# Handing layer 1's expert results to layer 2's attention batch by batch, and agreeing the maxima of a quantized attention through TensorE

## The chip, the cores and the metric

The kernel runs on one core of a Trainium2 chip. The metric is the device time of one execution in microseconds (us). A core has five engines that matter here: PE (TensorE, matrix products and transposes), DVE (VectorE), ACT (ScalarE), POOL (GpSimd) and SP (SyncE, which only issues transfers). Each works through its own list of instructions in order; an instruction waits until what it reads is there and what it overwrites is free, and everything behind it on the same engine waits with it. PEld is the loading of weights into PE, which overlaps its matmuls.

## The reference, cut to what matters

The whole is a decoder of four layers with three sublayers each, on X of 8 batches, 256 tokens and 256 features, always x = layernorm(x + sublayer(x)). The change touches the hand-over from the third sublayer of layer 1 (routed experts) to layer 2, the attention of layer 2, and its second sublayer, which is quantized.

```python
# layer 1, experts: each token takes the rows of its 4 experts, weighted
routed = zeros_like(x).at[t_s].add(expert_out[e_s, slot] * gate)
x = layernorm(x + routed + shared)
# layer 2, attention: 16 heads, causal; then the quantized sublayer
def bitnet_linear(x, W, b):
    w_scale = maximum(mean(abs(W)), 1e-05)
    qW = sign(W) * (abs(W) > 0.5 * w_scale)
    i_scale = maximum(max(abs(x)), 1e-08) / 127.0      # one maximum over ALL of x
    qx = clip(round(x / i_scale), -128.0, 127.0)
    return einsum('...i,oi->...o', qx, qW) * (w_scale * i_scale) + b
vis = bitnet_linear(dinov2_features, W_d2v, b_d2v)
image_embeds = bitnet_linear(vis, W_img, b_img)
fused = bitnet_linear(text_embeddings, W_txt, b_txt)   # text_embeddings is x
for Wa, ba in ((W_att0, b_att0), (W_att1, b_att1)):
    kv = bitnet_linear(image_embeds, Wa, ba)
    k = concatenate([kv, kv], axis=-1)
    attn = softmax(einsum('bse,bpe->bsp', fused, k) * inv_sqrt_e, axis=-1)
    fused = fused + 0.1 * einsum('bsp,bpe->bse', attn, k)
concatenated = concatenate([fused, broadcast(mean(image_embeds))], axis=-1)
h = relu(bitnet_linear(concatenated, W_f1, b_f1))
x = layernorm(x + bitnet_linear(h, W_f2, b_f2))
```

Six inputs of `bitnet_linear` need a maximum over everything: the context (called ctx in the code), vis, the image embeddings (img), x, the concatenation (cat) and the hidden layer (hid).

## The kernel before, in words

X stays in SBUF as 128 partitions by 16 tiles by 256 features (tile t holds tokens 128t to 128t+127; a batch is two tiles). `xT` is its transposed copy: four PE transposes (L175) and one ACT copy (L176) for two tiles. The sublayers run one after the other, but a planner orders the instructions on each engine by estimated costs and due times, so work of the next sublayer stands where an engine has room. Matrix products go through the helper `mm` (L134), and so many groups of the profile carry that line.

*Norms.* `finish_x` takes statistics with DVE (L165, L166), then 1/sqrt(variance) for two tiles by `rsqrt`, then writes X (L189). `rsqrt` has two forms: where `self.power` is set, two POOL instructions, an addition (L143) and a power (L145); otherwise eleven small DVE instructions (L148, L150, and three times L153, L154, L156). `POWER` lists the sublayers with the POOL form; the quantized sublayer is not among them.

*Experts of layer 1 to layer 2.* The 32 experts write their rows to DRAM (`yd1`). Inside the expert loop, `prepare_l2_xattn` also runs: it turns the weights of the quantized sublayer into -1, 0, 1 and computes vis, img and the transposed keys `l2x_kvT`. Afterwards `routed_batches` returns two functions to the attention: `gather(b)` fetches a batch's expert rows with eight indirect DMAs issued by POOL (helper at L953), `take(b)` multiplies the selection matrix with the gates (L1282, DVE), sums the rows by PE (L1291), adds to X (L1296) and norms. The buffer `ys` holds the rows of four tiles, that is two batches, by tile number modulo 4.

*Attention.* `attention16` projects a pair of batches (`pair`), then per batch: the largest score of each row (`largest16`, DVE reduces L499 and L515, lowered into q by L534 and L536), exponentials (`exps16`, ACT, L554), weighted sums (`sums16`, PE L603, then divisions on POOL L590, the addition with bias on POOL L612, and the norm). Scores of b+1 go between the exponentials of b. Before the first projection it gathers batches 0 and 1, takes both, and issues the gathers of 2 and 3 behind each take; later `gather(b + 4)` stands at the head of iteration b and `take(b + 3)` behind the second exponential step.

*Maxima.* `all_max` reduces along the free dimension with DVE (L1766) and over the 128 partitions with POOL's all-reduce (L1768). `step_of` makes the step, its inverse and the scales (L1776 to L1782), `quantize` rounds 512 columns with two DVE instructions (L1790, L1791), `bit_linear_T` multiplies and adds scale and bias (L1867).

*Quantized sublayer* (`l2_xattn`). x's maximum is taken of all of `xT` in one reduce over 128x4096. Then 16 calls of `bit_attend` (two rounds of eight batches): the keys' transpose (L1963, PE) and its copy (L1965, ACT), scores of two tiles (PE), the row maximum (L1971), subtraction (L1973), exponential (ACT), sum (L1976), reciprocal (L1977), multiplication (L1978), two transposes (L1981), copy (L1983), product (PE), and the addition to `fused` (L1987). Then the maximum of `fused` in one reduce (L1889), the maximum of the 8x256 averages (L1890), cat's all-reduce, 16 quantizations, a first pass over the hidden layer that keeps only maxima (`top`, L1921), hid's all-reduce, and four chunks of 512 tokens: hidden layer again, Relu on ACT (L1939), quantization, second product, addition to z (z = X + b2 on POOL, L1949; L1956 on DVE), norm.

## Time and profile before

| | |
|---|---|
| median of 3 runs | 2708.56 us (2705.01 to 2714.05) |
| profiled execution | 2698.26 us, its span 2696.5 us |
| mean granted TensorE clock | 0.886 of full speed |
| experts of layer 1 end, first gathers begin | 1108 to 1111 us |
| first projection of layer 2's attention | 1154.55 us |
| last write of X in that attention | 1408.12 us, 0.73 us long for both tiles |
| first multiplications with x's step | 1419.52 us |
| 16 calls of `bit_attend` | 1431.5 to 1473.6 us |
| maximum of fused | 1473.62 us, 4.42 us long |
| hid's all-reduce | 1516.78 us |
| last X of the quantized sublayer | about 1576 us |

Times of instructions count from the start of the span. A row of the timeline gives start, duration, engine, line, operation, output<-input with the names of the program, shapes, and in brackets the engine's idle time before it with what released it; "issue" is idle time for which the profile shows no cause. A group sums all instructions of one line and form: busy us, mean ns of one, and idle time ahead of them. The chain of waits is followed back from the last instruction of the span.

### The profile page before, as it was taken

What the parts mean: (1) busy time and instruction counts of PE and PEld (TensorE: products, weight loads), DVE (VectorE), ACT (ScalarE), POOL (GpSimd) and SP (SyncE); (2) the same over time, 40 slices, a digit from 0 to 9 for tenths busy, and PEclk for the clock granted to TensorE, in tenths of its full rate; (3) what the DMA queues carried; (4) which work ended last, traced back from release to release, by engine and by line L of the source; (5) the groups of instructions that cost most, each with busy time, mean ns of one, the idle gap of its engine ahead of it and who ended that gap; (6) DMA issues with size and microseconds to landing.
All of it is one profiled execution on the core that took longest, in us unless ns stands there. A gap on an engine that the chain in (4) does not pass through costs nothing.

```text
span 2696.5 us, 41126 instructions
## 1 busy us (share of the span) xinstructions
PE 2157.2 (80%) x14463; PEld 1564.6 (58%) x14463; DVE 1624.2 (60%) x5567; ACT 987.7 (37%) x2234; POOL 935.2 (35%) x980
## 2 busy tenths in 40 slices
PE   8988789699988688667976777778788778777796
PEld 5656678455565477334544355556667656565575
DVE  4764200566667575246667886758667676654675
ACT  2322233233433332123432343344435434343563
POOL 1021221311111134443110145665566555662122
PEclk9998799799988689778997888889889989887899
DMA  2002431200010137411010021111111111120000
GB/s 83 2 1 65 174 128 56 71 1 1 1 67 17 49 111 228 121 56 32 1 50 10 1 66 44 42 49 44 41 43 42 47 43 41 51 72 16 0 13 20
DMA packets 84173, 135.05 MB, mean 50 GB/s; under 512 B 33445, under 2 KB 53045, under 8 KB 82048
## 3 DMA queue, kind: packets, MB, share of 16 engines
q0 software_dynamic: 52288, 79.27, 10.0%
q1 hardware_dynamic: 28924, 49.45, 5.5%
q10 hardware_dynamic: 2756, 3.72, 0.4%
q8 instruction: 115, 1.88, 0.3%
q14 instruction: 90, 0.74, 0.1%
HBM read 242.90 MB, written 17.70 MB: 97 GB/s over the span
## 4 chain that ended last, share of the span: by engine, by line
PE 36%; DVE 22%; issue 10%; POOL 5%; ACT 4%; DMA 3%; another core or an unknown queue 3%; POOLq 0%; ACTq 0%; DVEq 0%
PE po L1498 5%; PE pp L134 4%; PE sc L134 4%; PE s L134 4%; DVE low L515 2%; DMA xe<-xd,take 2%; PE ph L134 2%; PE sc L482 2%; PE pt L134 2%; DVE low L499 2%; PE sc L603 2%; DVE junk L1446 1%; POOL rows L953 1%; DVE X L189 1%
## 5 line engine op out<-in xcount | busy, mean ns | idle before, releaser
L953 POOL DMA_INDIRECT rows<-in_l2f_table_dram,index x512 | 532.3, 1040 | 337.7 <-issue 121.5
L1498 PE MATMUL po<-rows,diag 128*128 128x256 f32 x768 | 231.8, 440 | 105.1 <-ACT diag L1497 68.1
L1446 DVE SCALAR_TENSOR_TENSOR junk<-rows,X 128x256 f32<-128x256 f32 x512 | 214.8, 420 | 53.4 <-DMA rows<-in_l2f_table_dram,index 32.4
L1498 PEld LDWEIGHTS po<-rows,diag 128*128 128x128 f32 x768 | 155.5, 216 | 156.4 <-ACT diag L1497 82.4
L134 PE MATMUL pp<-xT,w 128*128 128x256 f32 (+1 forms) x672 | 199.5, 436 | 30.6 <-issue 20.4
L134 PE MATMUL ph<-xeT,we 128*128 128x128 f32 x1248 | 182.1, 289 | 19.4 <-DMA we<-in_l0f_experts_dram,wrow 15.0
L590 POOL TENSOR_TENSOR aT<-sides,inv 128x256 f32<-128x256 f32 x64 | 46.7, 730 | 425.8 <-DVE sides L588 310.8
L134 PEld LDWEIGHTS ph<-xeT,we 128*128 128x128 f32 x1248 | 168.5, 199 | 39.3 <-DMA we<-in_l0f_experts_dram,wrow 16.3
L1497 ACT ACTIVATE diag<-ident,dots 128x128 f32<-128x128 f32 x384 | 134.3, 395 | 117.8 <-PE po L1498 48.1
L134 PEld LDWEIGHTS pp<-xT,w 128*128 128x128 f32 x672 | 139.5, 216 | 61.9 <-issue 25.8
L175 PE MATMUL pt<-ident,X 128*128 128x128 f32 x352 | 75.9, 330 | 107.0 <-DVE X L189 89.1
L953 POOL DMA_INDIRECT xe<-xd,take x87 | 85.0, 977 | 204.1 <-DVE y L1074 77.6
L176 ACT COPY xT<-pt 128x512 f32<-128x512 f32 x88 | 51.6, 586 | 271.6 <-PE pt L175 232.4
L175 PEld LDWEIGHTS pt<-ident,X 128*128 128x128 f32 x352 | 49.9, 164 | 140.3 <-DVE X L189 51.6
L134 PE MATMUL py<-we,hT 128*128 128x256 f32 x496 | 129.0, 384 | 0.9 <-DVE hT L1097 0.9
L1074 DVE TENSOR_TENSOR y<-py,we 128x256 f32<-128x256 f32 x23 | 9.8, 425 | 197.5 <-PE py L134 197.5
L554 ACT ACTIVATE e<-sc 128x512 f32<-128x512 f32 (+1 forms) x154 | 81.4, 602 | 103.0 <-PE sc L482 74.2
L1068 ACT ACTIVATE hT<-ph,we 128x128 f32<-128x128 f32 x184 | 65.7, 367 | 119.5 <-PE ph L134 87.9
L482 PE MATMUL sc<-kv,qv 32*128 32x128 f32 (+2 forms) x1448 | 103.9, 320 | 1.8 <-DVE qv L700 0.6
L189 DVE TENSOR_SCALAR X<-z,ln_mv,rs_y 128x256 f32<-128x256 f32 x176 | 68.3, 431 | 51.5 <-POOL rs_y L145 51.3
L482 PEld LDWEIGHTS sc<-kv,qv 32*128 32x128 f32 x1448 | 80.4, 190 | 31.4 <-issue 26.0
L482 PE MATMUL sc<-qv,kv 32*128 32x128 f32 (+2 forms) x1384 | 97.0, 343 | 0.1
(510 smaller groups left out, 5150.3 us busy)
## 6 DMA issues: line engine op xcount, KB each, us to landing
we<-in_l1f_experts_dram SPq DMA_DIRECT2D x32, 384.0 KB
yd<-y SPq DMA_DIRECT2D x32, 256.0 KB
rows<-in_l2f_table_dram,index POOLq DMA_INDIRECT x512
w<-in_l2x_w_dram SPq DMA_DIRECT2D x1, 4096.0 KB
yd<-y SPq DMA_DIRECT2D x23, 128.0 KB
X<-in_x_dram SPq DMA_DIRECT2D x8, 256.0 KB
xd<-X ACTq DMA_DIRECT2D x8, 256.0 KB
xd<-X SPq DMA_DIRECT2D x8, 256.0 KB
```

Of the source, the lines that this page charges most:

```text
L134: self.nc.tensor.matmul(out, lhsT=lhsT, rhs=rhs, start=n == 0, stop=n == last and bias is None)
L175: nc.tensor.transpose(pt[:, c, j, :], self.X[:, i0 + j * step, c * P : (c + 1) * P], self.ident)
L189: nc.vector.tensor_scalar(self.X[:, i, :], z[:, j, :], mv[:, j, 0:1], r[:, j : j + 1], ALU.subtract, ALU.mult)
L482: nc.tensor.matmul(sc[: shape[0], part], lhsT=lhsT, rhs=rhs, start=mask is None, stop=True, skip_group_check=True)
L499: nc.vector.tensor_reduce(low5[:, r, :, :, 0], sc, AX.X, ALU.max, negate=True)
L515: nc.vector.tensor_reduce(low4[:, r, :, 0], sc, AX.X, ALU.max, negate=True)
L554: lambda r, sc: nc.scalar.activation(e0[m][:n0, r], sc, AF.Exp),
L953: self.nc.gpsimd.indirect_dma_start(out=out, out_offset=None, in_=table, in_offset=bass.IndirectOffsetOnAxis(ap=index, axis=0), **({} if r ...
L1068: nc.scalar.activation(hT[:, g + f, :], ph[:, f, :], AF.Gelu, bias=b1[:, g + f : g + f + 1])
L1446: nc.vector.scalar_tensor_tensor(junk, row, 1.0, self.X[:, i, :], ALU.mult, ALU.mult, accum_out=out)
L1497: nc.scalar.activation(diag, self.ident, AF.Copy, scale=dots[:, k : k + 1])
L1498: nc.tensor.matmul(po, lhsT=diag, rhs=rows[:, k, D:], start=False, stop=g + k == H * K - 2)
```

## The change

1. `routed_batches` returns three functions instead of two. `first` gathers batches 0 and 1, takes both, and issues the gathers of batch 2 behind the take of batch 0; `second`, after the first projection, takes batch 2 and issues the gathers of batch 3; `inside(b)` takes b+3 and only then gathers b+4. Batch 1's rows lie in the second half of `ys`, those of all other batches in the first half, so that a batch's gathers follow its predecessor's sum. Norms of batches 0 and 1 take the DVE form of `rsqrt`.
2. `all_max` transposes the column of 128 maxima with PE, reduces the row with DVE, and spreads the one value over the partitions by a matmul with a row of ones. All six maxima use it.
3. x's maximum is collected by batches during layer 2's attention (`measure`, a reduce over 128x512 of X behind each norm), fused's during the second round of `bit_attend`.
4. The 16 transposes of the keys and their copies (now four of 128 columns by four) move from `bit_attend` to `prepare_l2_xattn`, into layer 1's expert loop; `l2x_kv` keeps them.
5. `bit_attend`: the negative scaled maximum becomes the bias of the exponential, which ACT takes from PSUM in two instructions that also give the sums; subtraction and sum on DVE go.
6. Loops over 512 columns become the outer ones in `quantized`, `bit_linear_T` and for the input of f1.
7. The quantized sublayer joins `POWER`.

```diff
@@ -84,6 +84,8 @@
         self.avg = self.const.tile([P, 2, B], F32, name="avg")
+        self.x_max = self.const.tile([P, B], F32, name="x_max")
         self.w_scale = self.const.tile([P, len(L2X)], F32, name="w_scale")
@@ -640,18 +643,10 @@
-        if ready:
-            gather, take = ready
-            for b in range(2):
-                gather(b)
-            for b in range(2):
-                take(b)
-                self.transpose_into_xT(2 * b, 1)
-                gather(b + 2)
+        first, second, inside = ready or (lambda: None, lambda: None, lambda b: (lambda: None,) * 3)
+        first()
         pair(0)
-        if ready:
-            take(2)
-            self.transpose_into_xT(4, 1)
+        second()
         for step in self.largest16(q[0], k[0], low[0], sizes, causal):
@@ -661,22 +656,21 @@
             here, e = self.exps16(q[b], k[b], sizes, causal, work)
-            if ready and b + 4 < B:
-                gather(b + 4)
+            early, late, last = inside(b)
+            early()
             for n, step in enumerate(here):
...
                     ahead[n]()
-                if n == 1 and ready and b + 3 < B:
-                    take(b + 3)
+                if n == 1:
+                    late()
                 if n == 0 and before:
...
                 before[1]()
-            if ready and b + 3 < B:
-                self.transpose_into_xT(2 * b + 6, 1)
+            last()
             values = vps[b // 2 % 2]
@@ -789,6 +783,12 @@
         nc = self.nc
+        def measure(b):
+            nc.vector.tensor_reduce(
+                self.x_max[:, b : b + 1], self.X[:, 2 * b : 2 * b + 2, :], AX.XY, ALU.max, apply_absolute_value=True
+            )
         wq, wkd, wku, wo, bku, bo, spare = w
@@ -810,7 +810,7 @@
-            self.attention16(project, low, vps, [P, P], True, wo, bo, work, ready=self.routed_batches(spare))
+            self.attention16(project, low, vps, [P, P], True, wo, bo, work, then=measure, ready=self.routed_batches(spare))
@@ -1273,9 +1273,13 @@
         def gather(b):
-            for t in (2 * b, 2 * b + 1):
+            for j in range(2):
+                t = 2 * b + j
                 for g in range(4):
-                    self.gather_rows(ys[:, t % 4, g, :], self.yd1, self.slot1[:, t, g : g + 1])
+                    self.gather_rows(ys[:, rows_at(b) + j, g, :], self.yd1, self.slot1[:, t, g : g + 1])
+        def rows_at(b):
+            return 2 if b == 1 else 0
@@ -1289,14 +1293,44 @@
                     nc.tensor.matmul(
-                        po[bands[g], j, :], lhsT=sel[:, j, g, :], rhs=ys[:, (2 * b + j) % 4, g, :],
+                        po[bands[g], j, :], lhsT=sel[:, j, g, :], rhs=ys[:, rows_at(b) + j, g, :],
                         start=True, stop=True, skip_group_check=True,
...
             nc.vector.tensor_tensor(x, po, x, ALU.add)
+            self.power = b > 1
             self.finish_x(2 * b, 1, x)
-        return gather, take
+            self.power = True
+        def first():
+            for b in range(2):
+                gather(b)
+            for b in range(2):
+                take(b)
+                self.transpose_into_xT(2 * b, 1)
+                if not b:
+                    gather(2)
+        def second():
+            take(2)
+            gather(3)
+            self.transpose_into_xT(4, 1)
+        def inside(b):
+            def late():
+                if b + 3 < B:
+                    take(b + 3)
+                if b + 4 < B:
+                    gather(b + 4)
+            def last():
+                if b + 3 < B:
+                    self.transpose_into_xT(2 * b + 6, 1)
+            return lambda: None, late, last
+        return first, second, inside
@@ -1759,14 +1793,19 @@
-    def all_max(self, parts, pool, name):
+    def all_max(self, parts, pool, name, bank=None):
...
         nc.vector.tensor_reduce(m, parts, AX.X, ALU.max, apply_absolute_value=True)
-        out = pool.tile([P, 1], F32, name=f"{name}_all")
-        nc.gpsimd.partition_all_reduce(out, m, P, bass_isa.ReduceOp.max)
-        return out
+        bank = bank or (lambda: self.ps_t.tile([P, 512], F32, name="pt"))
+        pt = bank()[:1, :P]
+        nc.tensor.transpose(pt, m, self.ident)
+        out = pool.tile([1, 1], F32, name=f"{name}_all")
+        nc.vector.tensor_reduce(out, pt, AX.X, ALU.max)
+        pt = bank()[:, :1]
+        nc.tensor.matmul(pt, lhsT=self.ones, rhs=out, start=True, stop=True)
+        return pt
@@ -1821,13 +1860,13 @@
-    def quantized(self, q, src, name, into, work, *weights):
+    def quantized(self, q, src, name, into, work, *weights, largest=None, bank=None):
         n = src.shape[2]
-        m = self.all_max(src.rearrange("p c n -> p (c n)"), into, name)
+        m = self.all_max(src.rearrange("p c n -> p (c n)") if largest is None else largest, into, name, bank)
         inv, scales = self.step_of(m, [q[x][1] for x in weights], into, name)
         dst = into.tile([P, 2, n], BF16, name="q_act")
-        for c in range(2):
-            for o in range(0, n, 512):
+        for o in range(0, n, 512):
+            for c in range(2):
                 e = min(o + 512, n)
@@ -1836,20 +1875,29 @@
         q = self.l2x_q = self.ternary(pool)
+        bank = lambda: ps.tile([P, 512], F32, name="pp")
         half = self.l2x_flat[:, 4096 : 4096 + 2 * NCTX]
         self.l2x_kvT = half.rearrange("p (c n) -> p c n", c=2)
         vis = pool.tile([P, 2, NCTX], F32, name="vis")
-        qc, (s,) = self.quantized(q, self.ctxT, "ctx", pool, pool, "d2v")
+        qc, (s,) = self.quantized(q, self.ctxT, "ctx", pool, pool, "d2v", bank=bank)
         self.bit_linear_T(vis, q["d2v"][0], qc, s, self.col("l2x_b_d2v"), ps)
         img = pool.tile([P, 2, NCTX], F32, name="img")
-        qv, (s,) = self.quantized(q, vis, "vis", pool, pool, "img")
+        qv, (s,) = self.quantized(q, vis, "vis", pool, pool, "img", bank=bank)
         self.bit_linear_T(img, q["img"][0], qv, s, self.col("l2x_b_img"), ps)
-        qi, scales = self.quantized(q, img, "img", pool, pool, "att0", "att1")
+        qi, scales = self.quantized(q, img, "img", pool, pool, "att0", "att1", bank=bank)
         for n in range(2):
...
             )
+        self.l2x_kv = self.l2x_flat[:SC, 6144:8192].rearrange("p (a n) -> p a n", n=P)
+        for n in range(2):
+            for b in range(0, B, 4):
+                pt = bank()[:SC].rearrange("p (a n) -> p a n", n=P)
+                for a in range(4):
+                    nc.tensor.transpose(pt[:, a, :], self.l2x_kvT[:, n, (b + a) * SC : (b + a + 1) * SC], self.ident)
+                nc.scalar.copy(self.l2x_kv[:, n * B + b : n * B + b + 4, :], pt)
         nc.vector.tensor_reduce(self.avg, img.rearrange("p c (b s) -> p c b s", s=SC), AX.X, ALU.add)
@@ -1857,8 +1905,8 @@
         n = src.shape[2]
-        for m in range(dst.shape[1]):
-            for o in range(0, n, 512):
+        for o in range(0, n, 512):
+            for m in range(dst.shape[1]):
                 e = min(o + 512, n)
@@ -1877,22 +1925,28 @@
             fused = pool.tile([P, 2, NTOK], F32, name="fused")
+            largest = pool.tile([P, B + 1], F32, name="largest")
+            nc.vector.tensor_reduce(largest[:, B:], avg, AX.XY, ALU.max, apply_absolute_value=True)
             if True:
                 with tc.tile_pool(name="x2a", bufs=3, space=PSUM) as ps:
-                    qx, (s,) = self.quantized(q, self.xT, "x", pool, work, "txt")
+                    qx, (s,) = self.quantized(q, self.xT, "x", pool, work, "txt", largest=self.x_max)
                     self.bit_linear_T(fused, q["txt"][0], qx, s, self.col("l2x_b_txt"), ps)
...
                         for b in range(B):
-                            self.bit_attend(fused, kvT[:, n, b * SC : (b + 1) * SC], b, work, ps)
-            largest = pool.tile([P, 2], F32, name="largest")
-            nc.vector.tensor_reduce(largest[:, 0:1], fused, AX.XY, ALU.max, apply_absolute_value=True)
-            nc.vector.tensor_reduce(largest[:, 1:2], avg, AX.XY, ALU.max, apply_absolute_value=True)
+                            self.bit_attend(
+                                fused, kvT[:, n, b * SC : (b + 1) * SC], self.l2x_kv[:, n * B + b, :], b, work, ps
+                            )
+                            if n:
+                                nc.vector.tensor_reduce(
+                                    largest[:, b : b + 1], fused[:, :, b * S : (b + 1) * S], AX.XY, ALU.max,
+                                    apply_absolute_value=True,
+                                )
             m = self.all_max(largest, pool, "cat")
             inv, (s1,) = self.step_of(m, [q["f1"][1]], pool, "cat")
             qf = pool.tile([P, 2, NTOK], BF16, name="q_act")
-            for c in range(2):
-                for o in range(0, NTOK, 512):
+            for o in range(0, NTOK, 512):
+                for c in range(2):
                     self.quantize(qf[:, c, o : o + 512], fused[:, c, o : o + 512], inv, work)
@@ -1956,24 +2010,22 @@
-    def bit_attend(self, fused, kvb, b, work, ps):
-        nc = self.nc
-        pt = self.ps_t.tile([SC, P], F32, name="pt")
-        nc.tensor.transpose(pt, kvb, self.ident)
-        kv = work.tile([SC, P], F32, name="kv")
-        nc.scalar.copy(kv, pt)
+    def bit_attend(self, fused, kvb, kv, b, work, ps):
+        nc = self.nc
         sc = ps.tile([P, 2, SC], F32, name="sc")
...
         nc.vector.tensor_reduce(mx, sc, AX.X, ALU.max)
+        nc.vector.tensor_scalar(mx, mx, -(D**-0.5), None, ALU.mult)
         e = work.tile([P, 2, SC], F32, name="e")
-        nc.vector.tensor_tensor(e, sc, mx.unsqueeze(2).to_broadcast([P, 2, SC]), ALU.subtract)
-        nc.scalar.activation(e, e, AF.Exp, scale=D**-0.5)
         total = work.tile([P, 2], F32, name="total")
-        nc.vector.tensor_reduce(total, e, AX.X, ALU.add)
+        for j in range(2):
+            nc.scalar.activation(
+                e[:, j, :], sc[:, j, :], AF.Exp, scale=D**-0.5, bias=mx[:, j : j + 1], accum_out=total[:, j : j + 1]
+            )
         nc.vector.reciprocal(total, total)
@@ -2140,7 +2192,7 @@
-POWER = ("l0_attn", "l0_xattn", "l1_attn", "l1_xattn", "l2_attn")
+POWER = ("l0_attn", "l0_xattn", "l1_attn", "l1_xattn", "l2_attn", "l2_xattn")
```

## The prediction

> **What bounds the kernel now.** I read the page's first part, then the chain that ended last (it names the work that sets the end, stage by stage), then busy time by stretches, groups and single instructions in the stages that the diff touches.
>
> ```profile
> PE 2157.2 (80%) x14463; PEld 1564.6 (58%) x14463; DVE 1624.2 (60%) x5567; ACT 987.7 (37%) x2234; POOL 935.2 (35%) x980
> ```
>
> TensorE (PE) leads with 80% of the span, but no step of the change lightens it by more than a few us. What the change can win are serial stretches, where the chain hops between engines. The first is the hand-over from layer 1's experts to layer 2's attention (columns: start, us, what):
>
> ```profile
> 1108.38 2.12 DMA yd<-y
> 1111.36 0.94 POOL w L953
> ...
> 1130.11 2.58 DMA w<-yd,w
> 1132.89 1.07 PE sc L1291 x2
> 1135.90 2.68 issue
> 1142.62 0.96 POOL w L953
> ...
> 1148.91 0.95 POOL w L953
> 1151.35 0.75 POOL rs_y L145
> 1152.65 1.24 PE pt L175 x4
> 1154.55 3.80 PE sc L134 x4
> ```
>
> The reader is to see POOL (GpSimd) in the middle of it: sixteen gathers of 0.95 us, a start every 1.25 us, before batch 0 and 1 are summed; eight more (batch 2's and half of batch 3's follow on the same queue) before POOL gives the second norm's root at 1151.35 and the first projection starts at 1154.55. The second kind of serial stretch is the agreement of a maximum over partitions (timeline; in brackets the idle time before and its releaser), together with two rows on a shared port, used under part 7:
>
> ```profile
> 1410.64 4.42 DVE L1766 TENSOR_REDUCE x_m<-xT 128x1 f32<-128x4096 f32 x1 [1.57 <-ACT xT L176]
> 1418.73 0.38 POOL L1768 PARTITION_ALL_REDUCE x_all<-x_m  x1 [10.64 <-issue]
> 1419.14 0.15 DVE L1776 TENSOR_SCALAR x_step<-x_all 128x1 f32<-128x1 f32 x1 [4.08 <-POOL x_all L1768]
> ...
> 1516.78 0.38 POOL L1768 PARTITION_ALL_REDUCE hid_all<-hid_m  x1 [5.83 <-issue]
> 1538.81 1.33 POOL L1949 TENSOR_TENSOR z<-X,b 128x512 f32<-128x512 f32 x1 [3.81 <-DVE X L189]
> 1538.92 1.50 DVE L1790 TENSOR_SCALAR quant<-h,hid_inv 128x512 f32<-128x512 f32 x1
> ```
>
> POOL's own work is 0.38 us; ahead of it lie 3.67 us (1415.06 to 1418.73) and 5.5 us (hid_m ends 1511.26) with nothing recorded. The third is the quantized attention of layer 2 and the chunks behind it (stretch, its us, then PE, PEld, DVE, ACT, POOL busy, clock granted to TensorE, DMA share, GB/s), with two groups of VectorE (DVE) and one of TensorE from there:
>
> ```profile
> 1431.50:1452.00 20.50, 17.72 (x122) 15.00 (x122) 16.63 (x50) 7.29 (x24) 0.00 (x0) 1.00 0.01 2
> 1518.00:1550.00 32.00, 23.81 (x128) 12.90 (x129) 31.19 (x111) 21.16 (x44) 4.19 (x3) 0.88 0.00 1
> ```
>
> ```profile
> L1973 DVE TENSOR_TENSOR e<-sc,mx 128x240 f32<-128x240 f32 x16 | 6.4, 400 | 0.1
> L1976 DVE TENSOR_REDUCE total<-e 128x2 f32<-128x240 f32 x16 | 6.2, 387 | 0.0
> ```
>
> ```profile
> L1963 PE MATMUL pt<-ident,w 128*120 128x128 f32 x15 | 4.2, 282 | 0.0
> ```
>
> In attention PE (86%) and DVE (81%) share the bound; in the chunks DVE is the bound (31.19 of 32 us).
>
> **The change part by part.** Sums are against the profiled execution: span 2696.5, 1.76 outside, 2698.26 in all; it lies 10.3 below the median 2708.56, and I put the sum onto the median. What a kernel without change would show moves by some 8 us (0.3%; the three times span 9).
>
> 1. *First gathers and norms.* Gathers of 0 and 1 still end at 1131.0 and land by 1132.7; b=1's sum 1.07 us to 1134; add, statistics and aggregation to 1135.9 as now. Then eleven small DVE instructions at 0.15 with a dependent hop of 0.04 each: 2.1, to 1138. X 0.74, four transposes 1.24, ACT's copy 0.59, to 1140.6, against 1154.55: **−13.9**. The order shows batch 2's gathers behind batch 0's sum, now on nobody's path: they end near 1141, POOL's code loading (7.5 us idle stands before its first power in the trace) to 1148.6, L612 2.5 to 1151; the third batch's sum is due about 1155 on PE. Cover: 4 us. If it is gone, the sum of batch 2 is late, −10 instead of −13.9.
>
> 2. *Later gathers.* All 64 gathers stay, SP's queue is untouched. In the order on POOL one more group of eight stands ahead of a norm's power (batch 6's, as batch 5's now). That stall is in the trace: X of a stalled batch waited 5.06 us, of another 1.13. Difference 3.9 at most, part of it behind PE's work: **+3** (0 to +6). A batch's gathers need 8×1.25+2.6 = 12.6 us; iterations are 27 to 39 us (sums at 1198.8, 1237.5, 1264.6), so they land in time.
>
> 3. *Maximum of x.* Now from X's last write (1408.85) to the step 1419.14: 10.3. After: one reduce over 128x512 (4.42/8 = 0.55, a 128x512 row from PSUM 0.69), a reduce of nine or eight values 0.15, a PE transpose 0.4, DVE 0.2, PE 0.3, hops: 2.4. **−7.9**. If PE stands in other transposes meanwhile, −6. The other seven reduces go into attention: 7×0.6 = 4.2 of DVE directly behind each norm, ahead of the next score reduces, which are on the chain (L499, L515): **+4** (0 to +5). The o-outer loops change little: DVE's order still has all sixteen quantizations first, so only the scores of batch 0 come earlier: **−1.2**; for the fused input 0.
>
> 4. *Layer 1's experts take on work.* 16 transposes ×0.27 = 4.3 of PE, four ACT copies (ACT is at 24% there, nothing), and three maxima through PE, in a stretch where PE is busy 89.11 of 100 us at full clock. PE works in order: while the small matmul waits for DVE's reduce, the expert matmuls queue behind it. Low end 0 (the chain there also waits for landing gathers, 3 to 5 us each), high end 4.3 + 3×1.5 = +9; I take **+5**.
>
> 5. *Attention.* 1431.48 to 1478.08 is 46.6 us with the 4.42 us maximum of fused behind it. Of DVE go 6.4 + 6.2; come 16×0.15 small scalings and 8×0.6 reduces: −5.4 with the 4.42 not counted. PE loses 4.2. ACT's two exponentials of 128x120 with sums replace one of 128x240 (0.40): 2×(0.30+0.19) = 1.0 a batch, which keeps ACT near 1.2 of the 2.3 us of a batch, no bound. PE then needs (17.72+16.16)/16 = 2.12 a batch less 0.27: 1.85; DVE 1.8 in the first round, 2.4 in the second. 8×1.95+8×2.4+4 of tail = 38.8: −7.8; I take **−7.5** (−3 if each batch keeps its latency of some 5 us through two buffers, −11 if DVE's parts overlap).
>
> 6. *Maxima of cat and hid.* cat now costs 0.64 from reduce to step, since POOL had nothing to load; through PE 1.5: **+0.9**. hid: 1511.04 to 1517.19 is 6.15, then 1.4: **−4.7**. *Rule against row:* the page "GPSIMD Engine Reference" of the Trainium skill sends a reduce over partitions to GpSimd (section 4.1) and also says (section 2.1) that the first call of freshly loaded code costs about 6 us that no instruction shows. By the first rule alone the change would lose: six times 1 us, +6. By the rows it is the second that counts here: 5.83 idle before hid's, 3.67 on x's path; but cat's shows the first where code was warm. Rows decide: −4.7 and +0.9.
>
> 7. *Norms of the quantized layer by POOL.* 88 small DVE instructions leave the 59 us of chunks. Interleaved they cost 0.07 to 0.15 each; at 0.10: −8.8. In come eight roots of 0.72 on POOL. *Rule against row:* "SBUF — State Buffer", section Who interferes with whom, has GpSimd and VectorE lock a shared port pair for a whole instruction. The row agrees: quant took 1.50 while z ran, 0.48 otherwise. By the rule every root could hold DVE 0.72: 8×0.72 = 5.8 back. I take half, 2.9: **−6** (0 to −10).
>
> Sum: −13.9 +3 −7.9 +4 −1.2 +5 −7.5 +0.9 −4.7 −6 = **−28.3**; 2708.6−28.3 = **2680**.
>
> **Rivals.** *Given back.* The expert stage pays 9, the norms give 0, attention only 3, the seven reduces 5, gathers 6: −28.3+4+6+4.5+1+3 = −9.8, **2699**. For it: PE at 89%, DVE at 97% beside a port that POOL locks. Against: these ends aren't all likely together.
>
> *The maxima don't get faster.* PE's transpose and matmul wait in order behind other PE work as long as POOL's loading took: −28.3+6+4.7−0.9 = −18.5, **2690**. Against: PE is busy 1.08 us in the 10.2 before the step.
>
> *Slower.* A batch's gathers now stand behind its predecessor's sum; if POOL reaches them only after a waiting L612 or division of the running batch, they land after PE, in order, has come to the next sum. Late up to 12.6 us, five batches (3 to 7): up to +63, **2743**; it decides from 28.3/5 = 5.7 us a batch. For it: POOL's queue has both kinds. Against: the shortest iteration is 27 us, and POOL works 18 of it (gathers 10, eight divisions of 0.73, L612 1.3, roots 1).
>
> *More than that.* Experts hide all (0), reduces 0, stall 0, attention −11, norms −10: −47.8, **2661**.
>
> **How the numbers follow.** Forecast 0.60 (its own range 2668 to 2692), given back 0.16, no faster maxima 0.09, slower 0.08, more 0.07. Range **2660 to 2702**: it holds all but the slower case and parts of the ends. Faster by over 0.3% (below 2700.4): 0.60+0.07+0.09+0.55×0.16 = 0.85; same 0.07 (the rest of the given back); slower 0.08.
>
> **What would show it.** Right: first projection near 1141 (counted in today's experts' end), no POOL idle before a maximum, step of x within 3 us of the last X, fused ready 39 us after its first scores, chunks at 12.5 us each instead of 14.2. Wrong: the experts end later than 1113; PE waits for L1291's gathers in attention; quant's mean above 0.6 us in the chunks; attention at 2.3 us a batch. A clock that falls as PE fills would take back a share of all.

## The result, and the profile after

The changed kernel takes 2688.68 us in the median of 18 runs (2668.23 to 2701.53); the kernel before, measured as often beside it, 2703.82 us (2695.43 to 2722.94). The ratio is 0.9937 with a 95% interval of 0.9920 to 0.9953: 17 us saved (13 to 22), where 28 were forecast. The profiled execution took 2687.66 us, its span is 2685.9 us. The first part of its page:

```profile
PE 2173.3 (81%) x14481; PEld 1569.7 (58%) x14481; DVE 1617.5 (60%) x5506; ACT 992.0 (37%) x2269; POOL 940.5 (35%) x986
```

Busy shares tell nothing here, as expected: the gain lies in serial stretches. The chain in the hand-over now reads as follows (start, us, what):

```profile
1113.60 0.95 POOL w L953
...
1119.87 2.64 DMA w<-yd,w
...
1131.27 7.86 another core or an unknown queue
1139.15 0.69 DVE X L1300
...
1146.15 0.74 DVE X L191 x2
1146.90 1.11 PE pt L177 x4
1148.04 0.59 ACT xT L178
1148.67 5.84 PE sc L136 x8
```

POOL's gathers and powers are gone from the end of this stretch; the first projection starts 35.07 us after the first gather instead of 43.19. But a row of 7.86 us stands in it that the forecast did not have. PE's records say that batch 1's sum ended at 1136.24; DVE adds it at 1139.15. The experiments return to it.

The maxima through PE, in the timeline (start, us, engine, line, ..., idle before):

```profile
1412.71 0.69 DVE L788 TENSOR_REDUCE x_max<-X 128x1 f32<-128x512 f32 x1
1413.44 0.16 DVE L1800 TENSOR_REDUCE x_m<-x_max 128x1 f32<-128x8 f32 x1
1414.15 0.28 DVE L1805 TENSOR_REDUCE x_all<-pt 1x1 f32<-1x128 f32 x1 [0.56 <-PE pt L1803]
1415.17 0.16 DVE L1815 TENSOR_SCALAR x_step<-pt 128x1 f32<-128x1 f32 x1 [0.73 <-PE pt L1807]
...
1500.87 0.28 DVE L1805 TENSOR_REDUCE hid_all<-pt 1x1 f32<-1x128 f32 x1 [0.36 <-PE pt L1803]
1501.62 0.16 DVE L1815 TENSOR_SCALAR hid_step<-pt 128x1 f32<-128x1 f32 x1 [0.47 <-PE pt L1807]
```

From X's last write to x's step it is 2.50 us now. Stage by stage, read off the starts of the same instructions in both profiles (forecast in the last column):

| stretch | before | after | change | forecast |
|---|---|---|---|---|
| experts: first row gather to first gather of results | 151.6 | 151.3 | -0.3 | +5 |
| first gather of results to first projection | 43.2 | 35.1 | -8.1 | -13.9 |
| first projection to last X of the attention | 253.6 | 263.3 | +9.7 | +3 and +4 |
| last X to x's step | 10.29 | 2.50 | -7.8 | -7.9 |
| x's step to first row maximum | 13.53 | 13.48 | -0.1 | -1.2 |
| first row maximum to cat's maximum | 45.4 | 39.4 | -6.0 | -7.5 |
| cat's maximum to step | 0.64 | 1.67 | +1.0 | +0.9 |
| cat's step to hid's maximum | 32.3 | 30.6 | -1.7 | 0 |
| hid's maximum to step | 6.15 | 1.33 | -4.8 | -4.7 |
| hid's step to last X of the sublayer | 59.3 | 59.2 | -0.1 | -6 |

The sum is -18.2 us. The span differs by -10.6, because stretches whose code is the same differ too: +2.5 before the experts' first gather, +0.2 behind the last X, +4.9 in layer 2's third sublayer (1104.2 and 1109.1). Over the eight experiments on chips of about the same speed that last stretch lies between 1097 and 1130 us, so one run's total says little; stretches of 30 to 60 us mostly repeat within 1 or 2 us.

In the attention of layer 2 and in the chunks the waits before X show what DVE does instead of working. Groups of DVE (busy us, mean ns | idle before, releaser), first of the kernel before, from 1154.5 to 1408.9 us, then of the changed kernel, from 1154 to 1412 us and from 1501.6 to 1560.8 us:

```profile
L189 DVE TENSOR_SCALAR X<-X,ln_mv,rs_y 128x256 f32<-128x256 f32 x12 | 4.6, 427 | 23.9 <-POOL rs_y L145 13.6 <-issue 10.3
...
L788 DVE TENSOR_REDUCE x_max<-X 128x1 f32<-128x512 f32 x7 | 4.8, 686 | 0.2
L191 DVE TENSOR_SCALAR X<-X,ln_mv,rs_y 128x256 f32<-128x256 f32 x12 | 4.6, 426 | 27.5 <-issue 13.8 <-POOL rs_y L147 13.6
...
L1829 DVE TENSOR_SCALAR quant<-h,hid_inv 128x512 f32<-128x512 f32 x32 | 18.1, 575 | 0.3
L191 DVE TENSOR_SCALAR X<-z,ln_mv,rs_y 128x256 f32<-128x256 f32 x16 | 5.9, 410 | 6.9 <-POOL rs_y L147 6.9
```

27.5 us before the routed batches' X, where it was 23.9: what is new is batch 6, whose root now stands behind six gathers of batch 7 (its X waits 4.78 us instead of 1.13). 6.9 us in the chunks: eight roots for which DVE, in order, waits. Before the change no X waited there.

### The profile page after: what moved, and what is told of

Read it like the earlier page. It is cut to its first block, busy times and chain, and to the rows that moved or that the text cites. A ratio compares the mean times of both kernels' runs of the same rounds, so it can differ in the third digit from the quotient of the medians.

```text
span 2685.9 us, 41132 instructions
## 1 busy us (share of the span) xinstructions
PE 2173.3 (81%) x14481; PEld 1569.7 (58%) x14481; DVE 1617.5 (60%) x5506; ACT 992.0 (37%) x2269; POOL 940.5 (35%) x986
## 4 chain that ended last, share of the span: by engine, by line
PE 38%; DVE 21%; issue 9%; POOL 4%; ACT 4%; another core or an unknown queue 4%; DMA 3%; POOLq 0%; ACTq 0%; DVEq 0%
PE po L1532 5%; PE pp L136 5%; PE s L136 4%; PE sc L136 4%; PE ph L136 2%; DVE low L517 2%; PE sc L484 2%; DMA xe<-xd,take 2%; PE pt L136 2%; DVE low L501 2%; PE sc L605 1%; DVE junk L1480 1%; DVE X L191 1%; PE s L1678 1%
## 5 line engine op out<-in xcount | busy, mean ns | idle before, releaser
L1532 PEld LDWEIGHTS po<-rows,diag 128*128 128x128 f32 x768 | 150.0, 209 | 144.4 <-ACT diag L1531 75.9
L136 PE MATMUL s<-xT,w 128*128 128x256 f32 x256 | 72.3, 444 | 38.3 <-issue 26.4
```

What stands on the lines that cost most here:

```text
L136: self.nc.tensor.matmul(out, lhsT=lhsT, rhs=rhs, start=n == 0, stop=n == last and bias is None)
L1532: nc.tensor.matmul(po, lhsT=diag, rhs=rows[:, k, D:], start=False, stop=g + k == H * K - 2)
```

## The experiments

Every kernel is the changed one with the edit shown, and each was timed beside the kernel before on its chip. Eight of the runs were on chips where the kernel before takes 2710 to 2728 us, the last four (from the second attempt at batch 2's gathers on) where it takes 2591; so only ratios and stretches are compared. The changed kernel's own ratio is 0.9937. The way from the first gather of results to the first projection is called the front.

**Norms of the quantized sublayer back on DVE.**

```diff
-POWER = (..., "l2_attn", "l2_xattn")
+POWER = (..., "l2_attn")
```

> The changed kernel with the quantized sublayer taken out of POWER again (its eight norms by eleven small DVE instructions). Theory: POOL's norms brought nothing because DVE, which works in order, stands 0.77 to 1.14 us before each X for the root (6.9 us over eight norms) and shares a port with POOL; the 59.2 us from hid's step to the last X stay 58 to 61. Rival: the norms saved their 6 us and another part of the change (the loop order, the softmax behind) lost as much there: the stretch grows to 64 to 66 us.

Measured: 57.8 us from hid's step to the last X, ratio 0.9939 (0.9911 to 0.9968). The theory holds, if anything too mildly: DVE's eighty-eight small instructions cost no more than POOL's eight roots. The rival's 64 to 66 us are excluded. In the ten profiles with these norms on POOL and X's writes in their place, the stretch takes 59.1 to 60.8 us, so this part of the change brings nothing and, against this run, costs 1 to 3 us. Groups of DVE in this run, from 1503.2 to 1561.2 us:

```profile
L1829 DVE TENSOR_SCALAR quant<-h,hid_inv 128x512 f32<-128x512 f32 x32 | 15.2, 480 | 0.4 <-ACT h L1993 0.2
L156 DVE TENSOR_TENSOR rs_a<-rs_a,rs_v 128x2 f32<-128x2 f32 x24 | 6.8, 285 | 0.2
```

The shared port does not explain it by way of the roots, during which DVE stands anyway. POOL's six additions z hold back DVE in both kernels. Here three of them meet a small L156 (285 ns in the mean where its neighbour L155 has 151, 3.2 us in all); in the changed kernel they meet `quant` and `qh` (575 and 475 ns instead of 480 and 421, 4.5 us in all).

**No per-batch maxima of X.**

```diff
-            self.attention16(..., then=measure, ready=...)
+            self.attention16(..., ready=...)
-                    qx, (s,) = self.quantized(q, self.xT, "x", pool, work, "txt", largest=self.x_max)
+                    qx, (s,) = self.quantized(q, self.xT, "x", pool, work, "txt")
```

> The changed kernel without the per-batch maxima of X; x's maximum comes from one reduce of 128x4096 over xT as before, then through PE. Theory: each of the seven reduces of 0.69 us stands on the chain behind its norm, so attention (first projection to last X, 263.3 us) gets 4 to 5 us shorter, and the way from last X to x's step grows from 2.5 to about 8.2 us (1.8 for transposes and copy, 4.42, 1.9): no net gain of this part. Rival: the reduces are hidden, attention stays at 263, and the part was worth 5 to 6 us.

Measured: attention 261.7 us, last X to step 7.61, ratio 0.9963 (0.9938 to 0.9988). Neither expectation is met. The last iterations are shorter by 0.5 to 0.7 us each (18.6 becomes 17.9 and 14.3 becomes 13.7, where the kernel before has 17.9 and 14.0), so the reduces do stand on the chain there; in the earlier ones they are covered. They cost 1.6 us (263.4 us of attention in another run on this chip that has them), the step saves 5.1: the collecting is worth 3.5 us, and it does not explain +9.7.

**The first part undone.**

```diff
-            return 2 if b == 1 else 0
+            return 2 * b % 4
-                if not b:
-                    gather(2)
+                gather(b + 2)
...
-            gather(3)
...
-                if b + 4 < B:
-                    gather(b + 4)
...
-            return lambda: None, late, last
+            return lambda: gather(b + 4) if b + 4 < B else None, late, last
...
-            self.power = b > 1
-            self.power = True
```

> The changed kernel with the first part undone: gathers of b+2 behind each of the first takes, of b+4 at the head of an iteration, all norms by POOL. Theory: first gather to first projection goes from 35.1 back to 43 us; attention behind it loses the extra stall of batch 6's norm (5.5 us) and is 257 to 258 us; net about +2.5. Rival: the attention's loss of 9.7 us comes from something else than the gathers' place (the measured reduces alone, or code fetched late): attention stays at 262 to 263 and the kernel is 8 us slower.

Measured: 42.9 us to the first projection, attention 257.6, ratio 0.9954 (0.9928 to 0.9980). The theory's two numbers are met. The attention's addition (z) of batch 3 came 27.7 us after that of batch 2 with the change, 23.5 here, 21.5 before: 4.2 us for batch 6's norm, which falls into this step, behind batch 7's gathers. So this part gives 8 us in front and takes 5.7 back behind it.

**Norms of routed batches 0 to 6 on DVE.**

```diff
-            self.power = b > 1
+            self.power = b > 6
```

> The changed kernel with the norms of batches 0 to 6 of the routed results by DVE, not only 0 and 1. Theory: DVE waits 4.4 to 6.5 us for the roots of batches 2 to 6 (26.3 in all) only because they stand on POOL behind a batch's gathers; the eleven small instructions take 2.1 us each, so 5 times about 3.2 = 16 us less DVE waiting, most of it on the chain: attention at 248 to 253 us instead of 263.3. Rival: the waits lie beside PE's or ACT's work and are replaced by another: attention stays above 260.

Measured: attention 264.2 us, ratio 0.9965 (0.9946 to 0.9984). My theory falls: taking the waits away from DVE did not shorten the attention. The timeline of this run around batch 6's norm shows one reason:

```profile
1305.39 0.96 POOL L953 DMA_INDIRECT w<-yd,w  x1 [0.30 <-issue]
...
1312.95 0.96 POOL L953 DMA_INDIRECT w<-yd,w  x1 [0.30 <-issue]
```

```profile
1311.05 0.77 DVE X L191 x2
1311.82 3.59 another core or an unknown queue
1315.41 2.48 DVE low L517 x4
```

(the second fence is the chain). X is written at 1311.82 instead of waiting for POOL, and then DVE stands 3.59 us before a reduce of PE's scores, until 2.5 us after the last gather was issued. With that the run's step from batch 2 to 3 is 29.4 us. Taken off, the step would be 25.8, still only 1.9 less than with POOL's norms: PE's and ACT's work fills the rest. The wait of an engine that the profile names was no measure of what its removal brings.

**The keys' transposes back in the attention, and 48 more of them in the expert loop.**

```diff
-        self.l2x_kv = ...   # and the loop with 16 transposes and 4 copies
+        pt = self.ps_t.tile([SC, P], F32, name="pt")      # in bit_attend
+        nc.tensor.transpose(pt, kvb, self.ident)
+        kv = work.tile([SC, P], F32, name="kv")
+        nc.scalar.copy(kv, pt)
```

> The changed kernel with the 16 transposes of the keys and their copies back in the quantized attention. Theory: attention loses about the PE time that comes back, 16 x 0.28 = 4.5 us, less what lay idle: first row maximum to cat's maximum goes from 39.4 to 41 to 44 us; the expert stage stays at 151 to 155. Rival: the transposes fit in PE's idle time beside the softmax, attention stays at 39 to 40.

```diff
-        for n in range(2):
+        for n in (0, 1) * 4:
             for b in range(0, B, 4):
```

> The changed kernel with the 16 transposes of the keys and their copies done four times over in layer 1's expert loop (48 more, 13 us of PE). Theory: PE waits for landing gathers in that loop and takes the transposes in that time; the expert stage stays within 3 us of 151 to 155. Rival: PE is the bound there, each transpose counts: 164 to 168 us.

Measured: with the keys back 39.9 us from the first row maximum to cat's, experts 153.6, ratio 0.9943 (0.9920 to 0.9966). That is the rival's number, but the same stretch of kernels without the edit lies between 37.8 and 41.6 us over all runs, so a cost below 2 us cannot be seen; 4.5 is excluded. With 64 transposes the experts took 157.0 us beside 153.2 to 155.1 in three other kernels on that chip: 2 to 4 of 13 us, the theory's side at its edge. The move costs about 1 us and brings 0 to 2. That leaves the leaner softmax and the maximum taken in pieces as the likely source of the attention's 6 us; they were not tried singly, and neither was the order of the loops.

**Maxima of x, cat and hid by POOL again.**

```diff
+        if bank is None:
+            out = pool.tile([P, 1], F32, name=f"{name}_all")
+            nc.gpsimd.partition_all_reduce(out, m, P, bass_isa.ReduceOp.max)
+            return out
-        bank = bank or (lambda: self.ps_t.tile([P, 512], F32, name="pt"))
```

> The changed kernel with the maxima of x, cat and hid through POOL's all-reduce again (ctx, vis, img stay with PE). Theory: code loading comes back where POOL has done other work before: last X to x's step 5 to 6 us instead of 2.5, hid 6.2 instead of 1.3, cat 0.6 instead of 1.7: 7 to 8 us in all. Rival: the idle time of POOL was a wait for something that the other parts removed: all three take 0.6 to 1 us and the kernel is 2 to 4 us faster.

Measured: 10.70, 0.65 and 7.51 us, ratio 0.9979 (0.9956 to 1.0002). The rival is dead, the theory too small. The rows of its timeline:

```profile
1426.01 0.16 DVE L1800 TENSOR_REDUCE x_m<-x_max 128x1 f32<-128x8 f32 x1
1435.55 0.38 POOL L1803 PARTITION_ALL_REDUCE x_all<-x_m  x1 [11.06 <-issue]
...
1526.70 0.38 POOL L1803 PARTITION_ALL_REDUCE hid_all<-hid_m  x1 [5.96 <-issue]
```

Without the 4.42 us reduce, the same POOL instruction starts 9.4 us after its input is there, where it was 3.7 us before the change. POOL had ended the last norm's root at 1424.49; counted from there it is 11.06 us, and 10.64 in the kernel before. For hid it is 5.83 us before and 5.96 here from POOL's last work, 5.5 and 6.9 from the input. So the silent time seems to run from POOL's last work of another kind, not from the input: the long reduce had covered most of x's. What fills it the profile does not record, and why it is longer for x than for hid stays open. Maxima through PE are worth 8.2 + 6.2 - 1.0 = 13 us once X's maximum is collected early, the largest single part of the change.

**Batch 2's gathers later.** A first attempt issued them ahead of batch 1's sum:

```diff
-            return 2 if b == 1 else 0
+            return 2 if b in (1, 2) else 0
```

> The changed kernel with batch 2's rows in batch 1's half of the buffer, so that its gathers follow batch 1's sum instead of batch 0's. In four profiles with the gathers of batch 2 running, DVE's add of batch 1 starts 2.9 to 6.7 us after PE's sum has ended (0.03 us where POOL gathers nothing then). Theory: POOL's running gathers hold DVE back there; with none running the add follows the sum within 0.2 us and first gather to first projection goes from 35 to 37 us down to 29 to 31. Rival: the delay belongs to DVE's own stream (its instructions come late), the gathers play no part: it stays at 3 to 7 us and 35 to 37.

In this kernel batch 1 is summed from batch 2's rows, since the gathers overwrite its half first, and the sum waits for them: 50.9 us to the first projection. It doesn't do what its expectation says and tells nothing but one point: PE's records end the sum at 1148.08, DVE adds it at 1158.80. The second attempt puts them behind the take:

```diff
                 self.transpose_into_xT(2 * b, 1)
-                if not b:
-                    gather(2)
+            gather(2)
```

> The changed kernel with batch 2's rows in batch 1's half of the buffer and its gathers issued behind batch 1's take, so that POOL has no gather under way while batch 1 is summed (batch 3's gathers follow at once on POOL, its rows lie in batch 0's half). In the profiles with gathers of batch 2 running, both DVE's add of batch 1 and ACT's copy of batch 0's transposes come 3 to 11 us after the end that PE's records show. Theory: outstanding gathers hold back what follows PE there; the add now follows the sum within 0.2 us and first gather to first projection is 29 to 32 us instead of 35 to 41. Rival: the delay is there whenever two batches are summed back to back before a pause of PE; it stays at 35 to 41.

Measured: 29.31 us to the first projection, attention 256.7, ratio 0.9906 (0.9877 to 0.9934). That looks like the theory's win, but two things spoil it. The timeline shows POOL gathering without a pause up to 1158 us: the planner moved batch 3's gathers, whose half is free, in front of batch 2's, so that gathers were under way during the sum after all. And this run was on a chip where the kernel before is 4 to 5% faster. So the changed kernel itself was run on such a chip:

> The changed kernel as it is, once more, beside the kernel that follows (the last two ran on a chip on which all kernels are some 4% faster). Theory: the delay behind PE's sum of batch 1 comes with the gathers under way, not with the chip: first gather to first projection is 35 to 41 us again, attention 263 to 267, chunks 59 to 60; ratio to the kernel before 0.993. Rival: it was the other chip that took the delay away: 29 to 31 us here too.

Measured: 29.27 us to the first projection, attention 258.5, ratio 0.9895 (0.9875 to 0.9916). The rival is right: on this chip the gathers of batch 2 run beside the sum and nothing is late. Its timeline (PE's sum, DVE's add and ACT's copy of the transposes behind it), and the same rows of the changed kernel's first profile:

```profile
1139.43 1.06 PE L1295 MATMUL sc<-w 128*32 128x256 f32 x2 [0.32 <-DMA w<-yd,w]
1140.53 0.69 DVE L1300 TENSOR_TENSOR X<-sc,X 128x512 f32<-128x512 f32 x1 [5.39 <-PE sc L1295]
1141.57 0.58 ACT L178 COPY xT<-pt 128x512 f32<-128x512 f32 x1 [23.78 <-PE pt L177]
```

```profile
1135.18 1.06 PE L1295 MATMUL sc<-w 128*32 128x256 f32 x2 [0.21 <-DMA w<-yd,w]
1139.15 0.69 DVE L1300 TENSOR_TENSOR X<-sc,X 128x512 f32<-128x512 f32 x1 [7.88 <-remote]
1146.86 0.59 ACT L178 COPY xT<-pt 128x512 f32<-128x512 f32 x1 [33.29 <-remote]
```

There 0.04 us lie between the sum's recorded end and the add, here 2.91; over the other runs on the slower chips 6.1, 3.4, 6.7, 5.3, 10.0 and 10.6. On chips of the same speed it was 0.03 to 0.04 us in the kernel before and with the first part undone, where POOL issues no gather at that moment. Gathers under way are not enough, though: batch 0's sum ends beside batch 1's gathers, and in the changed kernel's first profile too its add follows 0.04 us later (1126.22 and 1126.26). Nor are PE's results alone late. In that profile DVE also stood before small instructions of batch 1's norm that wait for DVE's own last result:

```profile
1144.75 0.16 DVE L156 TENSOR_TENSOR rs_a<-rs_a,rs_v 128x2 f32<-128x2 f32 x1 [1.24 <-DVE rs_a L155]
```

The end of the lateness goes with the gathers: in all eight profiles of the slower chips with 24 or more of them in a row, the last late instruction (ACT's copy, in the first attempt DVE's add) starts 4.3 to 5.2 us after POOL began to issue the last one. Nothing points to instructions that were fetched late: from 1125 to 1150 us the profile's DMA view has the gathers' queue alone. So it takes gathers under way and those chips. What exactly is held back, and what differs between the chips, was not found, and no run made the gathers later in fact, so whether that helps on the slower chips was not tried.

**Combinations.** The same front, with the old order of later gathers, and X's writes of the chunks deferred (the edits of the gathers are left out here):

```diff
...
+                        if f == 2:
+                            write(ready)          # X's writes of the chunk before
...
-                        self.finish(i, 1, z)
+                        ready.append((i, z, *self.norm_stats(z, 2)))
```

> The same front, together with the order of the kernel before for the later gathers (of b+4 at the head of iteration b), and in the quantized sublayer X's writes of a chunk deferred behind the first quantizations of the next chunk, so that DVE has work while POOL takes the root. Theory: front 29 to 32 us, attention 257 to 259 instead of 263.3, chunks 53 to 56 instead of 59.2: 12 to 16 us below the changed kernel. Rivals: DVE's wait for the root is replaced by the port that POOL locks (chunks 58 to 60), and the front's delay stays (35 and more): 4 to 6 us below it.

Measured: 29.3 us, attention 262.5, chunks 55.7, ratio 0.9925 (0.9896 to 0.9953). Batch 2's root now stands behind six gathers of batch 4 and starts 29 us after the projection, 20 us in the run before; the attention's first batch came after 85.0 us instead of 75 to 76. What the old order saves at batch 6 (23.7 us for the step there instead of 27.5) it more than loses here. The chunks do what was expected; the attention and the total do not, the kernel takes 2569 us beside 2566 of the changed kernel on a chip of this speed. With the gathers of the second attempt instead:

> The changed kernel with two repairs: batch 2's gathers behind batch 1's sum (as in the run before the last), and X's writes of the quantized sublayer's chunks deferred behind the first quantizations of the next chunk. Theory: front 29 to 30 us, attention 256 to 258, chunks and what follows to the next sublayer's first gather 1 to 2 us shorter than in the changed kernel: 12 to 16 us below the changed kernel on the same chip, ratio to the kernel before 0.987 to 0.989. Rival: the repairs of single stretches are given back later: 0.992 to 0.994.

Measured beside the changed kernel on the same chip: 2562.78 us against 2566.26, ratio to before 0.9885 (0.9863 to 0.9907) against 0.9895: not distinguishable, where 12 to 16 us were expected. The group of X's writes in its chunks:

```profile
L1990 DVE TENSOR_SCALAR X<-z,ln_mv,rs_y 128x256 f32<-128x256 f32 x16 | 9.0, 580 | 1.8 <-POOL rs_y L147 1.7
```

The wait for the root fell from 6.9 to 1.7 us, X's writes grew from 410 to 580 ns each; the chunks take 54.3 instead of 59.9 us, but the next sublayer's first gather follows after 20.3 instead of 16.9. Some 2 of 5.6 us stay. The front was 29.27 in both: on this chip there was nothing to repair, and the attention, expected 256 to 258, took 258.7 beside 258.5.

## Why the prediction was right, and where its sizes were off

The direction, the place of each gain and the range hold; 2688.68 lies inside 2660 to 2702, three fifths of the forecast 28 us came. That the total is off by no more is partly luck: the experts' +5 did not come, which made up for most of the 5.8 us missing in front, and the norms' -6 did not come either. Of the signs named, x's step (2.5 us behind the last X) and fused (39.4 us from the first row maximum to cat's) came as said; the first projection came 5.8 us later than said, and the chunks did not get shorter. By the steps:

- *Part 1, first gathers (-13.9).* The sum was right to 0.1 us on one chip: 29.27 measured, 29.2 forecast (1140.6 from 1111.36). In the profile beside the prediction it was -8.1, through 2.9 us by which batch 1's add came late and 2.9 us of gaps between the second norm's small instructions. The step assumed "b=1's sum 1.07 us to 1134; add ... as now"; the trace of before had batch 0's add on time beside gathers, but no gathers running beside batch 1's.
- *Parts 2 and 3, +3 and +4.* Together +9.7. The undone first part gives 5.7 of it to the gathers (one stalled norm more, within its +6), the run without the reduces gives them 1.6 instead of 4. The rest, some 2.4 us, I did not trace to a cause; on the other chip the attention is 258.5, so part of it may go with the late results.
- *Part 3, maximum of x (-7.9)* and *part 6 (+0.9, -4.7)*: -7.8, +1.0, -4.8. The rule that the first call of loaded code costs silent time carried these; the rule that sends such reduces to GpSimd fails here for x and hid and holds only for cat (0.65 us against 1.67). The page of the Trainium skill "GPSIMD Engine Reference" (section 2.1) has about 6 us for that first call; counted from POOL's last instruction the rows show 5.8 and 6.0 for hid, and 10.6 and 11.1 for x, where the measurement decides. They show the silence; that it is code being loaded no run here shows.
- *Part 4 (+5)* was too pessimistic: -0.3 here, at most 2 to 4 us for three times the work again. PE at 89% did not mean that PE was on the path: the chain there waits for landing gathers (4.45 us at 1092.84, for one).
- *Part 5 (-7.5)*: -6.0, of which the moved keys hold little; the rest was not taken apart.
- *Part 7 (-6)* is the step that failed. It weighed freed instructions against the locked port and left out the plainest term: DVE works in order and has X directly behind the aggregation, so each root is 0.77 to 1.14 us of standing still, 6.9 us in all. The 2.9 us that it set down for the roots at the port were not the term: roots run while DVE stands, and what the port takes through POOL's z grew by 1.3 us only (4.5 against 3.2). The small instructions freed some 7 us (an estimate: 6.9 + 1.3 less the 1.4 between 57.8 and 59.2), 0.08 each instead of 0.10. Together the part is worth -0.1, and undone it is 1.4 us faster.

On the chip of the last runs the ratio 0.9895 is a saving of 27 us (22 to 32) of 2591: the forecast's size, though by partly other terms.

## What to carry to other kernels

Where an all-reduce over partitions interrupts other GpSimd work, measure the silent time before it from that engine's last instruction, not from the input; a transpose, a reduce and a matmul with ones cost 1.3 to 1.7 us here, with no such silence. Moving a small step from an engine that is full to one that is idle pays only if the full engine has something else to do until the answer is back, so look at what stands next in its order. And run a change that hinges on a few microseconds of overlap on more than one chip.

## What the runs showed of the hardware that was not expected

On some chips, VectorE and ScalarE took up results of TensorE 2.9 to 10.7 us after their recorded end while indirect gathers were under way; on two other chips within 0.04 us, with the same kernel on one of them. The kernel before takes 2704 to 2728 us on the former and 2591 on the latter. Most of the difference lies in layer 2's third sublayer with its 512 gathers: 1097 to 1130 us against 990 to 996 in the experiments.

GpSimd was silent for 5.8 to 11.1 us before an all-reduce behind elementwise work, and for 6.8 to 7.5 us before the first elementwise instruction behind the experts and the first gathers (6.81 in the changed kernel, 7.53 in the kernel before). It was not before cat's all-reduce, ahead of which it had done nothing since x's, nor before the roots that stand between later gathers (0.04 us at 1307.31 in the changed kernel).
